# New prices for an offline instruction planner, and other places for the turns of the small expert groups

## The chip, the cores and the metric

The kernel runs on one core of a Trainium2 chip. The metric is the device time of one whole execution in microseconds (us), as the median of the runs. One execution was also taken by the hardware profiler; all rows and windows below are from it. Engines: PE is TensorE, DVE is VectorE, ACT is ScalarE, POOL is GpSimd, SP is SyncE; PEld is TensorE's weight load.

## The reference

The input x has 4 sequences of 1024 steps with 256 channels. Two residual blocks follow each other; LN is a layer norm without weights.

```python
x = x + LN(rec(LN(x)))        # px = h@Ws.T + bs; g = sigmoid(h@Wg.T + bg)
                              # state_t = tanh(px_t + state_{t-1});  out_t = g_t * state_t
x = x + LN(ffn(LN(x)))
# ffn: h = rms(x, n1_w); q, k, v of 16 heads of 16 columns; q, k rms-normed per head
#      x1 = x + causal_attention(q, k, v) @ wo.T      (first 64 columns of the addend are 0)
#      xf = rms(x1, n2_w); softmax gate over 4 experts, the best 2 kept, weights normed to 1
#      e0: gelu(xf@up)@down    e1: (silu(xf@w1) * (xf@w2))@down
#      e2: four layers with gelu    e3: three layers with gelu
#      return x1 + sum of the experts by weight       (first 64 columns of the addend are 0)
```

The recurrence over 1024 time steps is serial: each step adds and takes a tanh of 4 x 256 numbers.

## The kernel before

**Tiling.** Time is cut into 8 chunks of 128 steps (`NI`), each with all 4 sequences, so attention has 32 tiles `(i, b)` of 128 queries. After attention, each token's row goes to DRAM (`row_d`) and its number to the list of one of 6 expert pairs ("kinds", in the `order` 3, 0, 1, 2, 4, 5). Each kind is worked off in groups of 256 tokens, gathered from DRAM by index. What is left of a kind, at most 128 tokens, is its "tail": a small group of its own, run behind all kinds, under a branch on the count. In this run two of the six tails have tokens.

**Order.** Nothing is scheduled by the compiler here. The kernel is written as some twenty generators ("streams"), which yield `Op(engine, cost, prio, reads, slots, banks, lag, ahead)` before they issue an instruction. `Plan.run` keeps one waiting `Op` of each stream and picks the one with the least start time, less its `ahead`, then the least `prio`. It then moves that engine's planned clock:

```python
key = (t - op.ahead, op.prio, n)
...
self.clock[op.eng] = t + op.cost
self.end = t + op.cost + op.lag
```

`end` is when the result counts as ready for readers and for the buffers given back. So `cost` and `lag` (us) settle nothing but the order in which instructions stand on each engine; on the chip each engine runs its list in that order and waits for semaphores. The planner also knows the buffers (`slots`) and the 7 PSUM banks, and places an instruction only where it believes one free. `fill` puts small bf16 matmuls with no use but to keep PE busy (L417) into planned PE gaps of 0.8 us and more, between 60 and 420 us of planned time.

**Streams around the change**, in the order in which a chunk passes through them:
- projections (L534) and gates (L567): products for px and g, transposed input by `transposed` (L463, copies L472).
- `recurrence`: per step a POOL add (L583) into `s` and an ACT tanh (L586), with the best priority, -9.
- `before`: gated state, transposed into `pu` (L623), two layer norms (`moments` L447; rows L643), x1 in one of two `xns` buffers (also called xn), row to DRAM.
- `heads`: q, k product `pqk` (L711), pad copy (L718), squares (L724), norm product (L739), transposes (L798), copies of k (L751) and q (L762). `value_rows` makes v (L778, L787).
- scores: per step of up to 4 blocks of 128 keys, products "s" (queries by keys, for the row maxima) and "sT" (keys by queries, for exp), both L883, with `ahead` 0.3. `look_maxima`: DVE reduces (L968, L975).
- exps (L1024, ACT, up to 512 columns), masks on the diagonal (L1044, POOL), products av with v (L1065).
- `after`, per tile: av copied (avT, L1084), transposed on PE (L1091), divided (L1096, L1098), transposed (L1109), copied (L1114), product with wo (L1120), added into xn, which gives x2 (L1128). An `xns` buffer is given back when all four tiles of its chunk have passed here and `experts_input`.
- `experts_input`: squares (L1142), transposes, gate product, weights and row to DRAM; then the counts of each kind and the lists.
- experts: `fetch` (POOL indirect DMA, L1516), `turn` (DVE scale x, L1531; PE transposes T, L1538; ACT copy, L1544), `group` with products up (L1561) and down (L1581), activations (L1622 to L1638), outputs (DVE, L1649), and `last`: layer norm and add (L1662 to L1678), rows to `out` (POOL indirect DMA, L1681). A group's plan holds its own pieces and a list `then`: the next groups' fetches and turns. Its up products read what its own turn, planned in the group before, made. `turn` uses one PSUM bank for all, and a tail's turn uses the same buffer for x as the turn of a kind's first group. `groups` chooses `then`; further groups of a kind are nested in a branch (L1728), tails in the branches of L1742.

Of the kernel before, what the change touches and what calls it, by code (L numbers as in the profile page):

```python
# [15 lines left out]
PSUM = bass.MemoryType.PSUM  # L16
# [237 lines left out]
def sandwich(  # L254
# [188 lines left out]
    def moments(prio, tiles, tag, reads):  # L443

        mv = stat.tile([P, len(tiles), 2], F32, tag=tag, name=tag)
        for n, t in enumerate(tiles):
            yield Op("DVE", 0.6, prio, reads)  # L447
            st6 = stat.tile([P, 6], F32, tag="st6", name="st6")
            nc.vector.bn_stats(st6, t)
            nc.vector.bn_aggr(mv[:, n, :], st6)  # L450
        return mv

    def transposed(prio, srcs, reads, name, ahead=0.0):


        n = len(srcs)
        big_, *bs = yield Op(
            "PE", 0.25 * n + 0.1, prio, reads, [big], banks=NCC, lag=0.2, ahead=ahead
        )
        to = big.tiles[big_[1]]  # L460
        for cc in range(NCC):
            for b, src in enumerate(srcs):
                nc.tensor.transpose(  # L463
                    banks.tiles[bs[cc]][:, b * P : (b + 1) * P],
                    src[:, cc * P : (cc + 1) * P], ident,
                )
        done(name, "in PSUM")
        for cc, (eng, copy) in enumerate(
            (("ACT", nc.scalar.copy), ("DVE", nc.vector.tensor_copy))
        ):  # L470
            yield Op(eng, 0.65, prio, [ev(name, "in PSUM")])
            copy(to[:, cc, : n * P], banks.tiles[bs[cc]][:, : n * P])  # L472
            give(bs[cc])
            done(name, cc)
        return big_, [ev(name, cc) for cc in range(NCC)]
# [94 lines left out]
    def recurrence():  # L570

        prev = None
        for i in range(NI):
            st, _ = states(i)
            last = ev("st", i)
            for t in range(P):
                if prev is None:
                    yield Op("ACT", 0.21, -9.0, [last])
                    nc.scalar.activation(st[:, :, t], st[:, :, t], AF.Tanh)
                else:  # L580
                    yield Op("POOL", 0.21, -9.0, [last])
                    s = sp.tile([P, NCC * B], F32, tag="s", name="s")
                    nc.gpsimd.tensor_tensor(s, st[:, :, t], prev, ALU.add)  # L583
                    done("s")
                    yield Op("ACT", 0.21, -9.0, [ev("s")])
                    nc.scalar.activation(st[:, :, t], s, AF.Tanh)  # L586
                    if t == 0:
                        done("last read", i - 1)
                done("t")
                last = ev("t")  # L590
                prev = st[:, :, t]
                if t == MOST - 1:
                    done("most", i)
            done("rec", i)
# [5 lines left out]
    def before():  # L600


        for i in range(NI):
# [34 lines left out]
                r = power(z, "r1")  # L638
            done("r1", i)
            for b in range(B):  # L640
                row, = yield Op("DVE", 0.8, prio, [ev("r1", i), ev("x1in", i)], [rows])
                t = rows.tiles[row[1]]
                nc.vector.tensor_scalar(  # L643
                    t, pu[b], mv[:, b, 0:1], r[:, b : b + 1], ALU.subtract, ALU.mult
                )
                nc.vector.tensor_tensor(x1[:, b, :], t, x1[:, b, :], ALU.add)
                give(row)
                if b % 2:
                    give(pu_b[b // 2])
# [44 lines left out]
    def heads(i, bs):  # L694
# [9 lines left out]
        for k, b in enumerate(bs):  # L704
            pad, pb = yield Op(
                "PE", 1.9, prio, [*hT_, ev("once")], [pads], banks=1, lag=0.2
            )
            pad_of[i, b] = pad
            pqk = banks.tiles[pb]
            for cc in range(NCC):  # L710
                nc.tensor.matmul(  # L711
                    pqk, lhsT=hT[:, cc, b * P : (b + 1) * P], rhs=wqk[:, cc, :],
                    start=(cc == 0), stop=(cc == NCC - 1),
                )
            done("pqk", i, b)
            qk = pads.tiles[pad[1]].rearrange("p s h d -> p (s h) d")[:, :, 0:HD]
            yield Op("ACT", 0.69, prio, [ev("pqk", i, b)])
            nc.scalar.activation(  # L718
                qk, pqk.rearrange("p (h d) -> p h d", d=HD), AF.Copy, scale=r3[:, b : b + 1]
            )  # L720
            give(pb)
            sq_, = yield Op("ACT", 0.62, prio, (), [sqs])
            sq = sqs.tiles[sq_[1]]
            nc.scalar.activation(sq, qk, AF.Square)  # L724
            done("sq", i, b)
            if len(bs) > 1:
                yield from value_rows(i, b)
            yield Op("DVE", 0.62, prio, [ev("sq", i, b)])
            nc.vector.tensor_reduce(ss[:, k * 2 * H : (k + 1) * 2 * H], sq, AX.X, ALU.add)
            give(sq_)  # L730
# [2 lines left out]
        rq = newton(ss, f"rq{n}")  # L733
        for k, b in enumerate(bs):
            if len(bs) > 1:
                yield Op("DVE", 0.8, prio + b)
            pad = pads.tiles[pad_of[i, b][1]]
            qk = pad.rearrange("p s h d -> p (s h) d")[:, :, 0:HD]
            nc.vector.tensor_tensor(  # L739
# [5 lines left out]
            pb, = yield from heads_T(prio + b, pad, 1, [ev("pad", i, b)])  # L745
            done("pk", i, b)
            yield Op(
                "ACT", 0.69, prio + b,
                [ev("pk", i, b), *([ev("last read", i)] if i < NI - 1 else [])],
            )  # L750
            nc.scalar.activation(  # L751
                kT[:, b, :, i * P : (i + 1) * P],
# [5 lines left out]
            q, pb = yield from heads_T(prio + b, pad, 0, [ev("pad", i, b)], [qs])  # L758
            give(pad_of[i, b])
            done("pq", i, b)  # L760
            yield Op("ACT", 0.69, prio + b, [ev("pq", i, b)])
            nc.scalar.activation(  # L762
                qs.tiles[q[1]], banks.tiles[pb].rearrange("p (h q) -> p h q", q=P),
                AF.Copy, scale=qn_s,
# [7 lines left out]
    def value_rows(i, b):  # L772
        prio = 4.0 * i - 5.0
        to, hT_, r3 = hT_of[i]
        pb, = yield Op("PE", 1.0, prio, hT_, banks=1, lag=0.2)
        pv = banks.tiles[pb][:, : H * HD]
        for cc in range(NCC):
            nc.tensor.matmul(  # L778
                pv, lhsT=big.tiles[to[1]][:, cc, b * P : (b + 1) * P], rhs=wv[:, cc, :],
                start=(cc == 0), stop=(cc == NCC - 1),  # L780
            )
        done("pv", i, b)
        values_of[i] = values_of.get(i, 0) + 1
        if values_of[i] == B:
            give(to)
        yield Op("DVE", 0.46, prio, [ev("pv", i, b)])
        nc.vector.tensor_scalar(  # L787
            v_all[:, b, i, :, 0:HD], pv.rearrange("p (h d) -> p h d", d=HD),
            r3[:, b : b + 1], None, ALU.mult,
        )  # L790
        give(pb)
        done("v", i, b)
# [153 lines left out]
    def look_maxima():  # L946

        for step in steps:
# [7 lines left out]
            for p in (1, 0):  # L956
                for j in range(2):
                    for m0, m1, h0, h1, half in step.runs:
                        yield Op(
                            "DVE", 0.12 + 1.05e-3 * (m1 - m0) * P, step.at - 1.05,  # L960
                            [ev("s", step.key, p)],
                        )
                        pb = of_step["s", step.key, p][j]
                        if not step.added and step.blocks[m1 - 1][1] == i:
# [47 lines left out]
    def exps():  # L1012
        for step in steps:
            of_step["ex", step.key] = []
            for p in range(2):
                ex = None
                for j in range(2):
                    got = yield Op(
                        "ACT", 0.2 + 0.83e-3 * step.w, step.at, [ev("sT", step.key, p)],
                        [] if ex else [exs],  # L1020
                    )
                    ex = ex or got[0]
                    pb = of_step["sT", step.key, p][j]
# [7 lines left out]
    def masks():  # L1031
        for step in steps:
            for p in range(2):
# [1 line left out]
                    continue  # L1035
                m, _, several = step.diagonal
                for j in range(2) if several > 1 else (slice(0, 2),):
                    yield Op("POOL", 0.72 if several > 2 else 0.42, step.at, [ev("e", step.key, p)])
                    e = exs.tiles[of_step["ex", step.key][p][1]][:, j, : step.w]
                    if several > 1:  # L1040
                        d, pattern = on_diagonal(e, step), [[0, several], [1, P]]
# [35 lines left out]
    def after(ns):  # L1077

        for n in ns:
            i, b = tiles[n]  # L1080
            prio = n + 1.5
            ahead = GATES_FIRST if n == NT - 1 else 0.0
            yield Op("DVE", 0.69, n - 0.5, [ev("av", n)])
            nc.vector.tensor_copy(avT, av)  # L1084
            done("av free", n)
            row, pb = yield Op(
# [3 lines left out]
            for hc in range(NHC):  # L1090
                nc.tensor.transpose(pa[:, hc * P : (hc + 1) * P], avT[:, hc, :], ident)  # L1091
            done("pa", n)
            yield Op("DVE", 0.7, prio, [ev("pa", n)])
            pa = pa.rearrange("p (h d) -> p h d", d=32)
            rs = stat.tile([P, H, 1], F32, tag="rs", name="rs")
            nc.vector.reciprocal(rs, pa[:, :, HD : HD + 1])  # L1096
# [12 lines left out]
                nc.tensor.transpose(pt[:, cc, :], ao[:, cc * P : (cc + 1) * P], ident)  # L1109
            give(row)  # L1110
            done("aoT0", n)
            yield Op("ACT", 0.39, prio, [ev("aoT0", n)])
            aoT = tees.tiles[to[1]]
            nc.scalar.copy(aoT, pt)  # L1114
            give(pb)
# [7 lines left out]
                )  # L1123
            give(to)
            done("po", n)
            yield Op("DVE", 0.36, prio, [ev("po", n)])
            xn = xns.tiles[xn_of[i][1]]
            nc.vector.tensor_tensor(xn[:, b, M:], po, xn[:, b, M:], ALU.add)  # L1128
            give(pb)
# [2 lines left out]
    def experts_input(chunks):  # L1132

        for i in chunks:
# [2 lines left out]
            xn = None  # L1137
            ss = stat.tile([P, B], F32, tag="ss2", name="ss2")
            for b in range(B):
                row, = yield Op("ACT", 0.6, prio, [ev("x2", i, b)], [rows])  # L1140
                xn = xns.tiles[xn_of[i][1]]
                nc.scalar.activation(  # L1142
                    rows.tiles[row[1]], xn[:, b, :], AF.Square, accum_out=ss[:, b : b + 1]
# [256 lines left out]
def experts(  # L1400
# [294 lines left out]
    def groups(c, g):  # L1695
# [6 lines left out]
        then = [fetch(c, g + 2)]  # L1702
        if g == 0:
            then += [fetch(kind(n + 2), 0), fetch(kind(n + 2), 1)]
            for before in [order[n - 1]] if n else []:
                then.append(fetch(before, TAIL, 1.0))
            if n + 1 == KINDS:
                then.append(fetch(c, TAIL, 1.0))
            else:
                then.append(turn(kind(n + 1), 0))  # L1710
        if more:
            then.append(turn(c, g + 1))
# [27 lines left out]
    for n, c in enumerate(order):  # L1740
        hint(f"tail{n}", KINDS + c, 0)
        with tc.If(n_of[KINDS + c] > 0, preferred_fallthrough_block=True, label=f"tail{n}"):  # L1742
            group(c, TAIL, [turn(c, TAIL)])


# [57 lines left out]
```

## Time and profile before

| what | value |
|---|---|
| median of 3 runs | 1471.9 us (1470.63 to 1476.9) |
| profiled execution | 1470.96 us |
| its span, first to last instruction | 1469.2 us |
| mean granted TensorE clock | 0.947 |
| PE busy | 1311.5 us, 89% |
| DVE, ACT, POOL busy | 896.5, 705.7, 465.5 us |
| fillers (L417) on PE | 38.6 us |
| recurrence, first to last tanh | 17.6 to 741.0 us |
| first exp to last exp | 147.7 to 1028.3 us |
| first tail's x to the end | 1426.94 us to 1469.2 us |

Some 1.8 us of the execution lie around the span. In a row of a profile, the source line and engine come first, then output and inputs by their names in the program, shapes, the count, busy time, the mean of one in ns, and the idle time of the engine before these instructions with what ended most of it. In a timeline the start and the duration come first. In windows the stretch, its length, and for each engine its busy time with the count, then the granted TensorE clock as a share of full speed. Matmuls may be merged into one line where they follow each other.

### The profile page before, as it was taken

Reading aid. Unit: us, or ns where it says so; the run is one execution under the profiler, and the core shown is the slowest. Engines: PE = TensorE matmul, PEld = TensorE weight load, DVE = VectorE, ACT = ScalarE, POOL = GpSimd, SP = SyncE. Lnnn points to the kernel's source line nnn. Section 1 sums busy time; section 2 is a strip of 40 time slices with the busy share of each in tenths; the row PEclk is TensorE's granted clock in tenths of the full one; section 3 lists DMA queues with packets and bytes.
Section 4 is the critical chain, followed back from the end, with each engine's and each line's share of the span. In section 5 each row is a group of like instructions: output and inputs, shape, how many; then the busy total and the mean of one; then the engine's idle time right before and its main releaser. Section 6 shows DMA issues by size and latency. Waiting matters only on the chain. (4 is left out here: it accounts for less than half of the span.)

```text
span 1469.2 us, 43267 instructions
## 1 busy us (share of the span) xinstructions
PE 1311.5 (89%) x17455; PEld 1020.3 (69%) x17470; DVE 896.5 (61%) x2738; ACT 705.7 (48%) x2144; POOL 465.5 (32%) x1466
## 2 busy tenths in 40 slices
PE   4578797988999998999999999999899999999964
PEld 2235455666676676687677677878688889888764
DVE  5567568599688778778877987784614312113311
ACT  2345545655765765776665455657222222223211
POOL 2433534535444444334311101101233321214321
PEclk8799989999998989998999999999999999999987
DMA  3010010001010000001000100131122120103210
GB/s 128 23 50 2 4 42 17 16 3 46 3 31 17 3 22 28 3 3 46 3 4 5 45 3 4 38 105 62 55 84 64 54 66 26 40 23 83 55 43 5
DMA packets 35917, 49.57 MB, mean 34 GB/s; under 512 B 7638, under 2 KB 27862, under 8 KB 35670
## 3 DMA queue, kind: packets, MB, share of 16 engines
q1 hardware_dynamic: 28774, 25.20, 5.6%
q0 software_dynamic: 6624, 20.62, 5.0%
q8 instruction: 147, 2.41, 0.7%
q14 instruction: 100, 0.82, 0.2%
q10 hardware_dynamic: 272, 0.52, 0.1%
HBM read 32.87 MB, written 13.46 MB: 32 GB/s over the span
## 5 line engine op out<-in xcount | busy, mean ns | idle before, releaser
L1024 ACT ACTIVATE ex<-bank 128x512 f32<-128x512 f32 (+1 forms) x592 | 325.9, 582 | 153.4 <-PE bank L883 87.5
L883 PE MATMUL bank<-keys,q 32*128 32x128 f32 x4608 | 351.9, 293 | 17.4 <-ACT q L762 4.1
L583 POOL TENSOR_TENSOR s<-keys 128x8 f32<-128x8 f32 x1023 | 223.4, 218 | 384.8 <-ACT keys L586 374.1
L883 PE MATMUL bank<-q,keys 32*128 32x128 f32 x4608 | 333.9, 292 | 5.4 <-ACT ex L1024 2.8
L883 PEld LDWEIGHTS bank<-q,keys 32*128 32x128 f32 x4608 | 272.6, 191 | 75.7 <-issue 41.9
L586 ACT ACTIVATE keys<-s 128x8 f32<-128x8 f32 x1023 | 218.5, 214 | 212.1 <-POOL s L583 209.5
L883 PEld LDWEIGHTS bank<-keys,q 32*128 32x128 f32 x4608 | 292.2, 193 | 37.0 <-DVE nm L975 6.3
L975 DVE TENSOR_REDUCE nm<-bank 128x1 f32<-128x512 f32 (+4 forms) x336 | 203.0, 639 | 53.7 <-PE bank L883 44.5
L968 DVE CUSTOM_DVE_ANT_0 bank<-bank,late 128x512 f32<-128x512 f32 (+2 forms) x320 | 188.3, 622 | 48.7 <-PE bank L883 47.4
L1044 POOL TENSOR_SCALAR_AFFINE_SELECT ex<-ex 128x256 f32<-128x256 f32 (+1 forms) x240 | 102.7, 429 | 262.4 <-ACT ex L1024 261.4
L1065 PE MATMUL av<-ex,values 128*17 128x128 f32 x4608 | 175.0, 282 | 3.1 <-issue 1.2
L1561 PE MATMUL bank<-values,keys 128*128 128x256 f32 x568 | 133.5, 381 | 5.9 <-PEq L1728 3.0
L1065 PEld LDWEIGHTS av<-ex,values 128*17 128x17 f32 x4608 | 110.0, 99 | 40.3 <-issue 16.4
L1622 ACT ACTIVATE keys<-bank 128x256 f32<-128x256 f32 (+1 forms) x136 | 50.4, 371 | 149.8 <-PE bank L1561 149.7
L1561 PEld LDWEIGHTS bank<-values,keys 128*128 128x128 f32 x568 | 105.8, 190 | 21.7 <-issue 3.5
L1561 PE MATMUL bank<-keys 128*128 128x256 f32 x384 | 84.8, 379 | 0.0
L1561 PEld LDWEIGHTS bank<-keys 128*128 128x128 f32 x384 | 73.0, 190 | 9.9
L534 PE MATMUL bank<-big,wsg 128*128 128x512 f32 x128 | 64.0, 646 | 5.9 <-ACT big L472 5.9
L711 PE MATMUL bank<-wqk,big 128*128 128x512 f32 x128 | 65.7, 642 | 3.2 <-ACT big L472 3.2
L1649 DVE SCALAR_TENSOR_TENSOR rwnext<-av,rwnext 128x192 f32<-128x192 f32 x24 | 8.9, 414 | 93.4 <-PE av L1581 93.4
L1622 ACT ACTIVATE hid<-bank 128x256 f32<-128x256 f32 x66 | 25.3, 383 | 84.5 <-PE bank L1561 84.5
L1669 POOL TENSOR_SCALAR z<-mv 128x2 f32<-128x2 f32 (+1 forms) x18 | 4.1, 227 | 187.7 <-DVE mv L1663 178.4
(265 smaller groups left out, 1788.2 us busy)
## 6 DMA issues: line engine op xcount, KB each, us to landing
row_d<-xn SPq DMA_DIRECT2D x16, 512.0 KB
xn<-in_x SPq DMA_DIRECT2D x8, 512.0 KB
xc<-in_x SPq DMA_DIRECT2D x7, 512.0 KB
keys<-in_e_l SPq DMA_DIRECT2D x2, 1024.0 KB
keys<-in_e_w SPq DMA_DIRECT2D x2, 512.0 KB
keys<-in_e_down SPq DMA_DIRECT2D x2, 384.0 KB
wsg<-in_w_sg ACTq DMA_DIRECT2D x1, 512.0 KB
xc<-in_x SPq DMA_DIRECT2D x4, 128.0 KB
```

The source lines that it names most:

```text
L534: nc.tensor.matmul(pb, lhsT=wsg[:, cc, half * C + dc * P : half * C + (dc + 1) * P], rhs=lnT[:, cc, :], start=(cc == 0), stop=(cc == NCC - 1),
L583: nc.gpsimd.tensor_tensor(s, st[:, :, t], prev, ALU.add)
L586: nc.scalar.activation(st[:, :, t], s, AF.Tanh)
L711: nc.tensor.matmul(pqk, lhsT=hT[:, cc, b * P : (b + 1) * P], rhs=wqk[:, cc, :], start=(cc == 0), stop=(cc == NCC - 1),)
L883: nc.tensor.matmul(banks.tiles[pbs[j]][:, m * P : (m + 1) * P], lhsT=k if kind == "sT" else q, rhs=q if kind == "sT" else k, start=(m == 0 ...
L968: nc.vector.tensor_tensor_reduce(out=s_, in0=s_, in1=late[:, 4 * P - w :], scale=-1.0, scalar=FMAX, op0=ALU.add, op1=ALU.min, accum_out=by ...
L975: nc.vector.tensor_reduce(by_slot[:, half, h0:h1, 2 * p + j], banks.tiles[pb][:, m0 * P : m1 * P].rearrange("p (h w) -> p h w", h=h1 - h0) ...
L1024: nc.scalar.activation(exs.tiles[ex[1]][:, j, : step.w], banks.tiles[pb][:, : step.w], AF.Exp)
L1044: nc.gpsimd.affine_select(out=d, in_=d, pattern=pattern, compare_op=ALU.is_ge, fill=0.0, base=0, channel_multiplier=-1,)
L1065: nc.tensor.matmul(av[32 * j : 32 * j + HD + 1, hc, :], lhsT=v_all[:, b, kb, 4 * hc + j, :], rhs=exs.tiles[ex[j // 2][1]][:, j % 2, m * P ...
L1561: nc.tensor.matmul(hb[0].tiles[hb[1]][:, :w_], lhsT=w[:, j, m * P : (m + 1) * P], rhs=src[:, j, :w_], start=(j == 0), stop=(j == nk - 1),)
L1622: nc.scalar.activation(to, src, AF.Gelu)
```

## The change

**Prices.** The costs of the ACT, DVE and POOL pieces of the first part of the kernel (up to the experts' lists) are lowered, a few raised, and a `lag` is added to most, so that what an instruction occupies its engine and what passes until its result can be read count apart. PE's prices, the priorities and the dependencies stay. The expert groups' own prices stay too.

**Turns of the tails.** Before, the first group of each kind but the first fetched the rows of the tail of the kind before (the last kind also its own), and each tail's own group began with its turn. After, in the first group of the kind at place n of the order: n = 1 fetches the tails of the places 0, 1 and 2; n from 2 on that of place n + 1. Their turns are planned there as well: n = 2 turns tails 0 and 1, n = 3 tail 2, n = 4 tail 3, n = 5 tails 4 and 5. All six are turned, whether the tail has tokens or not, and a tail's group holds no turn.

The diff, with the places between left out:

```diff
-            yield Op("DVE", 0.6, prio, reads)
+            yield Op("DVE", 0.53, prio, reads, lag=0.08)
...
-            yield Op(eng, 0.65, prio, [ev(name, "in PSUM")])
+            yield Op(eng, 0.5, prio, [ev(name, "in PSUM")], lag=0.1)
...
-                    yield Op("POOL", 0.21, -9.0, [last])
+                    yield Op("POOL", 0.16, -9.0, [last], lag=0.07)
-                    yield Op("ACT", 0.21, -9.0, [ev("s")])
+                    yield Op("ACT", 0.11, -9.0, [ev("s")], lag=0.11)
...
-                row, = yield Op("DVE", 0.8, prio, [ev("r1", i), ev("x1in", i)], [rows])
+                row, = yield Op("DVE", 0.92, prio, [ev("r1", i), ev("x1in", i)], [rows], lag=0.08)
...
-            yield Op("ACT", 0.69, prio, [ev("pqk", i, b)])
+            yield Op("ACT", 0.58, prio, [ev("pqk", i, b)], lag=0.1)
-            sq_, = yield Op("ACT", 0.62, prio, (), [sqs])
+            sq_, = yield Op("ACT", 0.55, prio, (), [sqs], lag=0.1)
...
-                yield Op("DVE", 0.8, prio + b)
+                yield Op("DVE", 0.61, prio + b, lag=0.08)
...
-                "ACT", 0.69, prio + b,
-                [ev("pk", i, b), *([ev("last read", i)] if i < NI - 1 else [])],
+                "ACT", 0.58, prio + b,
+                [ev("pk", i, b), *([ev("last read", i)] if i < NI - 1 else [])], lag=0.1,
...
-            yield Op("ACT", 0.69, prio + b, [ev("pq", i, b)])
+            yield Op("ACT", 0.58, prio + b, [ev("pq", i, b)], lag=0.1)
...
-        yield Op("DVE", 0.46, prio, [ev("pv", i, b)])
+        yield Op("DVE", 0.39, prio, [ev("pv", i, b)], lag=0.07)
...
-                            "DVE", 0.12 + 1.05e-3 * (m1 - m0) * P, step.at - 1.05,
-                            [ev("s", step.key, p)],
+                            "DVE", 0.1 + 1.0e-3 * (m1 - m0) * P, step.at - 1.05,
+                            [ev("s", step.key, p)], lag=0.08,
...
-                        "ACT", 0.2 + 0.83e-3 * step.w, step.at, [ev("sT", step.key, p)],
-                        [] if ex else [exs],
+                        "ACT", 0.05 + 0.84e-3 * step.w, step.at, [ev("sT", step.key, p)],
+                        [] if ex else [exs], lag=0.12,
...
-                    yield Op("POOL", 0.72 if several > 2 else 0.42, step.at, [ev("e", step.key, p)])
+                    yield Op("POOL", 0.6 if several > 2 else 0.37, step.at, [ev("e", step.key, p)], lag=0.1)
...
-            yield Op("DVE", 0.69, n - 0.5, [ev("av", n)])
+            yield Op("DVE", 0.6, n - 0.5, [ev("av", n)], lag=0.08)
...
-            yield Op("DVE", 0.7, prio, [ev("pa", n)])
+            yield Op("DVE", 0.62, prio, [ev("pa", n)], lag=0.08)
...
-            yield Op("ACT", 0.39, prio, [ev("aoT0", n)])
+            yield Op("ACT", 0.27, prio, [ev("aoT0", n)], lag=0.12)
...
-            yield Op("DVE", 0.36, prio, [ev("po", n)])
+            yield Op("DVE", 0.27, prio, [ev("po", n)], lag=0.08)
...
-                row, = yield Op("ACT", 0.6, prio, [ev("x2", i, b)], [rows])
+                row, = yield Op("ACT", 0.4, prio, [ev("x2", i, b)], [rows], lag=0.1)
...
         then = [fetch(c, g + 2)]
         if g == 0:
             then += [fetch(kind(n + 2), 0), fetch(kind(n + 2), 1)]
-            for before in [order[n - 1]] if n else []:
-                then.append(fetch(before, TAIL, 1.0))
-            if n + 1 == KINDS:
-                then.append(fetch(c, TAIL, 1.0))
-            else:
+
+            if n:
+                got = range(3) if n == 1 else (n + 1,)
+                turned = {2: (0, 1), KINDS - 1: (KINDS - 2, KINDS - 1)}.get(n, (n - 1,) if n > 1 else ())
+                then += [fetch(kind(k), TAIL, 1.0) for k in got]
+                then += [turn(kind(k), TAIL) for k in turned]
+            if n + 1 < KINDS:
         if more:
...
         with tc.If(n_of[KINDS + c] > 0, preferred_fallthrough_block=True, label=f"tail{n}"):
-            group(c, TAIL, [turn(c, TAIL)])
+            group(c, TAIL, [])
```

## The prediction, made before the changed kernel ran

> **What bounds the kernel now.** I read the page's busy times and costliest groups first, then stretches of the span, then the recurrence's line alone in the same stretches, then the timeline at the group boundaries that the second part of the change touches.
>
> ```profile
> PE 1311.5 (89%) x17455; PEld 1020.3 (69%) x17470; DVE 896.5 (61%) x2738; ACT 705.7 (48%) x2144; POOL 465.5 (32%) x1466
> L1024 ACT ACTIVATE ex<-bank 128x512 f32<-128x512 f32 (+1 forms) x592 | 325.9, 582 | 153.4 <-PE bank L883 87.5
> L583 POOL TENSOR_TENSOR s<-keys 128x8 f32<-128x8 f32 x1023 | 223.4, 218 | 384.8 <-ACT keys L586 374.1
> L586 ACT ACTIVATE keys<-s 128x8 f32<-128x8 f32 x1023 | 218.5, 214 | 212.1 <-POOL s L583 209.5
> ```
>
> PE is busy 89%, an average over stages that differ. The 1023 steps of the recurrence alternate between POOL (L583) and ACT (L586): each waits for the other. With nothing else on ACT in between, one step takes 0.522 us in the trace. The stretches below are cut at exps (L1024): first exp of a time chunk to its last ("chunk"), and last exp to the next chunk's first ("gap").
>
> ```profile
> core 0: us, PE busy (x) PEld busy (x) DVE busy (x) ACT busy (x) POOL busy (x), PEclk, DMA share, GB/s
> 159.30:245.60 86.30, 67.79 (x477) 43.52 (x479) 62.70 (x216) 42.88 (x177) 33.98 (x147) 0.90 0.09 26
> 292.80:323.60 30.80, 27.13 (x346) 18.78 (x346) 28.50 (x89) 16.33 (x68) 12.55 (x54) 1.00 0.01 2
> 424.10:521.20 97.10, 90.39 (x1603) 68.48 (x1605) 76.83 (x244) 64.50 (x216) 43.34 (x157) 0.93 0.07 19
> 531.80:645.00 113.20, 106.82 (x2016) 81.24 (x2016) 89.34 (x267) 75.40 (x248) 45.16 (x172) 0.93 0.06 17
> 645.00:647.00 2.00, 1.56 (x36) 1.26 (x32) 1.81 (x4) 1.44 (x6) 0.98 (x4) 1.00 0.03 8
> ```
>
> In a chunk PE is 93 to 94% busy. In the gap 159.3 to 245.6 it is idle for 18.5 us, filler matmuls included. The gap at 645 hardly exists. The recurrence alone in the gaps (first number behind the window is its length, then ACT busy with its count):
>
> ```profile
> 159.30:245.60 86.30, 30.54 (x143) 0.90 0.09 26
> 292.80:323.60 30.80, 11.15 (x53) 1.00 0.01 2
> 645.00:647.00 2.00, 0.47 (x3) 1.00 0.03 8
> ```
>
> So a gap is as long as the steps ordered into it: 143 steps x 0.522 plus what other ACT operations add makes 85.2 (measured 86.3); 53 make 31.8 (30.8). Gaps of few steps are those in which attention of the next chunk was ready.
>
> **Part A, the prices.** Durations do not change, nor any instruction's count (fillers aside): only the order. The new prices are near what the trace shows start to start (an exp of 512 columns 476 ns, now 0.48 for 0.625; the pad copy 570 to 585, now 0.58). PE's prices, among them 1.9 for L711's product, stay. So the question is what order results, and I take it from the instruction lists of both kernels. Recurrence steps between the last exp of a chunk and the first of the next, chunk 0 first: before 143, 53, 40, 20, 3, 0, 0; after 166, 41, 113, 2, 93, 0, 0. Exps ahead of the last step: 298 before, 240 after, of 592. The reason is in the order too: with cheap exps and reduces, scores (which have 0.3 us of "ahead") are always ready first, and PE work between the last av product of a tile and its avT transposes grows from 3.5 to 12 us in the median. So x2 is done later, xn's two slots come free later, and the next chunks' heads come late: the first L718 of chunk 3 is at step 585 where it was at 548, of chunk 5 at 919 for 820. In those gaps PE has only heads, projections and leftovers.
>
> Price of the gaps after: steps x 0.522 plus the trace's mean surplus for each ACT operation between steps (L718 0.91, L724 0.15, L751 0.35, L762 0.37, L1142 0.29, L472 0.31, L1114 0.33, L567 0.2, L1191 0.15). Gap 0: 86.7 + 11.9 for 33 operations = 99. Gap 1: 25 by steps, 32.5 us of PE work, so 33. Gap 2: 59.0 + 11.5 for 30 operations = 70. Gap 3: 1. Gap 4: 48.5 + 8.8 for 23 = 57. The last two 2.5 and 1. Sum 264, measured before 154: +110. Without any surplus the gaps after sum to 232: +78.
>
> Price of the chunks: PE work (each matmul at its busy time in the trace, 894 us in all, the same in both) moves from chunks to gaps. In the eight chunks it was 6.7, 41.9, 65.8, 88.7, 104.4, 121.9, 142.5, 114.8 (686.7; they took 726.4, so 39.7 us are stalls); it becomes 6.7, 33.0, 50.3, 78.7, 80.4, 107.8, 147.8, 109.5. At each chunk's own ratio these take 11, 37, 59.4, 86.2, 87.1, 112.3, 146, 106.8 = 645.8: -80.6. So gaps and chunks net +29, or -3 at the bare pace.
>
> Covers: PE work between first score product and sT grows from 9.4 to 14.9 us in the median, and cases with under 1.5 us between an exp and its av fall from 8 to 5. With fewer steps in the chunks this can take some of the 39.7 us of stalls; the ratio has already taken 8, and I give another 12 (rather under a third), with 0 and 25 as bounds. Against it, the cover between the gate's product and the counts falls from 26.4 to 1.9 us, and that chain takes 5.8 us in the trace (1043.78 to 1049.60): +4. Part A: 29 - 12 + 4 = +21. The fillers go from 154 to 159; 37 now stand together behind chunk 0's first transposes, 10.3 us at the 0.28 us that one keeps PE busy (38.6 us / 139 records), in a wait of 14.7 us for the row norms (90.8 to 105.5): nothing, unless that wait shrank by 4.
>
> The row 159.3 to 245.6, a gap with idle PE, has the clock 0.90; the packed one at 292.8 has 1.00. [...]
>
> **Part B, the turns.** Read at kind 2's first group, and at the two tails that run:
>
> ```profile
> 1187.27 0.60 PE L1538 MATMUL bank<-ident,values 128*128 128x128 f32 x4
> 1187.47 0.74 DVE L1649 SCALAR_TENSOR_TENSOR rwfirst<-bank,rwfirst 128x192 f32<-128x192 f32 x2 [2.64 <-PE bank L1581]
> 1187.91 0.58 ACT L1544 COPY values<-bank 128x512 f32<-128x512 f32 x1 [2.45 <-PE bank L1538]
> 1188.55 1.13 PE L1561 MATMUL bank<-values,keys 128*128 128x256 f32 x4 [0.67 <-ACT values L1544]
> 1426.94 0.35 DVE L1531 TENSOR_SCALAR values<-rwtail 128x256 f32<-128x256 f32 x1 [5.63 <-DVEq L1742]
> 1427.44 0.66 PE L1538 MATMUL bank<-ident,values 128*128 128x128 f32 x2 [10.95 <-DVE values L1531]
> 1428.13 0.37 ACT L1544 COPY xtail<-bank 128x256 f32<-128x256 f32 x1 [13.77 <-PE bank L1538]
> 1442.21 0.66 PE L1538 MATMUL bank<-ident,values 128*128 128x128 f32 x2 [3.65 <-DVE values L1531]
> ```
>
> Turns share one bank and, in part, one buffer, and the next kind's own turn already stands last in the group. Kind 2's last down product ends at 1187.27, and the next product starts 1.28 later. After, the order at this end is on PE T2, down, T2, T4, T4, on DVE x, outputs, x2, moments, x2 (T2, T4: transposes of one or two tiles). So behind the last down come outputs 0.74, moments 0.53, x 0.61, T4 0.60, copy 0.59, then x, T4 and copy again (1.80): with hops about 5.35, +4.1. Kind 3: T2, down, T4, T4 for T4, down, T4: 3.3 for 1.33, +2.0. Kind 4 +0.25, the last kind +0.6. Sum +6.95. Three row fetches more than one needs in kind 1 (9 for 7, 1.27 us of POOL each) delay rows by 2.5 us that have 6 in hand: nothing.
>
> Gains: at the first tail PE has walked the untaken branches by 1425.03, and DVE, ACT and PE then need x, T and copy until 1428.56. Without them a product can start at 1425.7: -2.85. At the second, PE is done with the first tail at 1438.57, but DVE's x waits behind that tail's closing chain until 1441.71, and the first product starts at 1443.33: -4.76. Together -7.6. Part B: -0.7, between -6 (turns hidden) and +2.
>
> **Sum.** The profiled execution took 1470.96, 0.9 below the median 1471.9. 1470.96 + 21 - 0.7 = 1491.
>
> **Rivals.** 0.5%, 7.4 us, is about what a measurement of this kernel can tell from no change.
> (1) Forecast: starved gaps lengthen the attention by more than the chunks return. Surplus full or half, stalls 0 to 25 off: 1482 to 1504. 0.62.
> (2) Faster: the surplus of ACT operations is mostly waiting on PE (L718 waits for L711) or contention that thinner stretches lack, so gaps run bare (-3), and the chunks lose a third or more of their 40 us of stalls (-12 to -20), the tails give their -1 to -6: 1450 to 1462. It decides if the gaps' steps come under 0.54 us. For it: the smallest surplus of an exp is 0.05, its mean 0.26. 0.13.
> (3) No net change, gaps bare and nothing more, or a cancelling of both: 1466 to 1479. 0.12.
> (4) Worse: the sum of the chunks is too kind, because their PE stalls do not shrink with their work (+8 on the ratio), and idle gaps cost clock (0.90 instead of 1.00 on 90 us of PE work in gaps 2 and 4: +9): 1505 to 1512. 0.13.
> The range 1464 to 1508 leaves out most of (2) and half of (4). Likeliest case alone: 1482 to 1504.
>
> **What would show it.** Right: some 113 tanh steps and 70 us between the exps of chunks 2 and 3, 93 steps and 57 us between 4 and 5, PE idle there for 15 to 25 us each; chunk 5's first exp near 690 (was 647), though the recurrence ends near 690 (was 741); attention's last exp near 1050 (was 1028); kind 2's first group 4 us longer; first tail product 2.9 and second 4.8 us sooner than the kinds' end would give. Wrong: gap steps at 0.53 us, or chunks 4 to 6 shorter than 87, 112 and 146 us.

## The result, and the profile after

| | median us | ratio to the kernel before, 95% interval |
|---|---|---|
| before | 1471.27 (4 runs) | |
| after | 1496.34 (4 runs) | 1.0163 [1.0141, 1.0185] |

The change costs 25 us. The profiled execution of after took 1495.79 us with a span of 1494.0 (before 1469.2), PE is busy 1335.6 us of it, again 89%, and the mean clock is 0.939 (0.947). The 24.7 us between the spans divide at the last exp: 17.5 ahead of it (1045.9 us, before 1028.3), 7.2 behind.

The stretches of after, cut at the exps as in the prediction (columns as there): the gaps behind chunks 0, 2 and 4, and between the last two, chunk 3.

```profile
core 0: us, PE busy (x) PEld busy (x) DVE busy (x) ACT busy (x) POOL busy (x), PEclk, DMA share, GB/s
157.70:253.90 96.20, 78.28 (x552) 49.34 (x552) 71.86 (x236) 48.68 (x204) 40.56 (x172) 0.93 0.08 23
377.20:448.20 71.00, 55.81 (x495) 39.43 (x487) 55.05 (x190) 36.63 (x148) 30.94 (x120) 0.86 0.09 24
448.20:528.70 80.50, 79.03 (x1596) 60.64 (x1600) 62.78 (x177) 58.84 (x203) 36.80 (x147) 0.96 0.01 3
618.30:678.80 60.50, 50.23 (x493) 38.05 (x491) 49.85 (x140) 29.25 (x121) 26.54 (x100) 0.77 0.09 28
```

The gap behind chunk 2 was 22.7 us and is 71.0; that behind chunk 4 was 2.0 and is 60.5. PE is idle for 15.2 and 10.3 us of them (the first numbers, less PE's busy time). Chunk 3 with the gap ahead of it paid is 98% busy. The recurrence alone (window, ACT busy with its count, clock) has 113 and 93 steps in these gaps:

```profile
377.20:448.20 71.00, 23.91 (x113) 0.86 0.09 24
618.30:678.80 60.50, 19.71 (x93) 0.77 0.09 28
```

Why the next chunk wasn't ready is seen in SP's queue: the row of chunk k - 2 goes out with x2 (L1149), and only when its transposes have read it can the load of chunk k (L607) take the same xn buffer. First the kernel before, for chunks 3 and 5, then after (start, duration of the issue):

```profile
332.39 0.36 SPq L1149 DMA_DIRECT2D row_d<-xn  x1
336.89 0.38 SPq L607 DMA_DIRECT2D xn<-in_x  x1
...
544.60 0.43 SPq L1149 DMA_DIRECT2D row_d<-xn  x1
548.92 0.38 SPq L607 DMA_DIRECT2D xn<-in_x  x1
```

```profile
341.16 0.36 SPq L1149 DMA_DIRECT2D row_d<-xn  x1
354.78 0.38 SPq L607 DMA_DIRECT2D xn<-in_x  x1
...
563.32 0.37 SPq L1149 DMA_DIRECT2D row_d<-xn  x1
580.83 0.53 SPq L1006 DMA_DIRECT2D q<-top  x1
581.47 0.52 SPq L607 DMA_DIRECT2D xn<-in_x  x1
```

Chunk 3's load comes 17.9 us later, chunk 5's 32.6. Of the latter 18.7 are a later x2, and 13.8 the longer way from the row to the load (18.2 us for 4.3): the transposes of x2 stand late in PE's list too (L463, at 579.8 us; before at 547.3). SP's own list adds little: q<-top (L1006), which stands ahead of the load, is issued at 580.83, just as the transposes end. All exps of chunk 4 are through at 618.3, but chunk 5's first product L711 needs x1, and its first pad copy (L718) is at 609.0 (before 578.1).

Behind the last exp, the end of kind 2's first group (timeline: start, duration; in brackets the engine's idle time and what ended it):

```profile
1208.76 0.38 PE L1538 MATMUL bank<-ident,values 128*128 128x128 f32 x2
1209.18 0.37 ACT L1544 COPY xtail<-bank 128x256 f32<-128x256 f32 x1 [2.41 <-PE bank L1538]
1210.24 0.61 DVE L1531 TENSOR_SCALAR values<-rwfirst 128x256 f32<-128x256 f32 x2
1210.74 0.72 PE L1538 MATMUL bank<-ident,values 128*128 128x128 f32 x4 [1.60 <-DVE values L1531]
1212.14 1.08 PE L1538 MATMUL bank<-ident,values 128*128 128x128 f32 x4 [0.68 <-ACT values L1544]
1213.90 1.65 PE L1561 MATMUL bank<-values,keys 128*128 128x256 f32 x3 [0.68 <-ACT values L1544]
```

The chain is the one foretold: the transposes right behind the last down product start at 1208.76, and the next product starts 5.1 us later (before 1.28). What follows was not foretold; the windows of the same place, clock third from the right:

```profile
1206.00:1210.00 4.00, 3.14 (x21) 2.88 (x19) 1.39 (x4) 1.02 (x3) 0.00 (x0) 1.00 0.00 0
1210.00:1214.00 4.00, 1.90 (x9) 1.24 (x9) 2.94 (x11) 1.17 (x2) 1.14 (x3) 0.78 0.00 0
1214.00:1218.00 4.00, 4.00 (x10) 3.19 (x11) 1.10 (x3) 0.67 (x2) 1.76 (x2) 0.50 0.09 33
1218.00:1222.00 4.00, 4.00 (x18) 3.46 (x17) 0.00 (x0) 1.25 (x4) 2.22 (x3) 0.87 0.43 120
```

PE is full from 1213.90 on, but the clock is halved (0.50): 10 matmuls of L1561 in 4 us, where the same line has 20 from 1222.00 to 1226.00, at a clock of 1.00. Cut more finely, the granted clock is 1.00 up to 1212.2, 0.50 from 1212.3 to 1219.0, in the middle of the chain and behind it, and 1.00 again from 1219.1 on. Before, the clock is 1.00 from 1180 to 1204 us, around the same end.

A last place, in kind 1's first group, where three tails are fetched:

```profile
1153.51 0.95 POOL L1516 DMA_INDIRECT rwtail<-row_d,tails  x1 [0.30 <-issue]
...
1155.57 0.41 DVE L1675 TENSOR_SCALAR rwfirst<-rwfirst,mv,r 128x256 f32<-128x256 f32 x1 [6.68 <-POOL r L1670]
...
1157.41 0.41 DVE L1632 SCALAR_TENSOR_TENSOR tnext<-tnext,bank 128x256 f32<-128x256 f32 x1
...
1157.87 4.97 PE L1561 MATMUL bank<-values,keys 128*128 128x256 f32 x20 [2.27 <-DVE tnext L1632]
```

POOL issues the last fetch, then makes r of the layer norm; DVE waits 6.68 us for r with the norm and x, and the piece that takes the tanh of the *next* products (L1632) stands behind them in DVE's list. PE waits 2.27 us for that.

### The profile page after: what moved, and what is told of

It is laid out like the page before. It is cut to its first block, busy times and chain, and to the rows that moved or that the text cites. A ratio compares the mean times of both kernels' runs of the same rounds, so it can differ in the third digit from the quotient of the medians.

```text
span 1494.0 us, 43375 instructions
## 1 busy us (share of the span) xinstructions
PE 1335.6 (89%) x17483; PEld 1039.6 (70%) x17483; DVE 900.7 (60%) x2742; ACT 709.1 (47%) x2148; POOL 468.5 (31%) x1466
## 5 line engine op out<-in xcount | busy, mean ns | idle before, releaser
L1024 ACT ACTIVATE ex<-bank 128x512 f32<-128x512 f32 (+1 forms) x592 | 320.3, 582 | 140.2 <-PE bank L883 71.3
L883 PE MATMUL bank<-q,keys 32*128 32x128 f32 x4608 | 320.0, 290 | 7.8 <-ACT ex L1024 5.2
L883 PEld LDWEIGHTS bank<-q,keys 32*128 32x128 f32 x4608 | 261.7, 189 | 74.5 <-issue 40.8
L975 DVE TENSOR_REDUCE nm<-bank 128x1 f32<-128x512 f32 (+4 forms) x336 | 202.8, 639 | 52.2 <-PE bank L883 42.3
L1561 PE MATMUL bank<-values,keys 128*128 128x256 f32 x568 | 139.6, 394 | 6.7 <-PEq L1730 2.9
L1561 PEld LDWEIGHTS bank<-values,keys 128*128 128x128 f32 x568 | 109.8, 197 | 24.8 <-issue 3.4
L1561 PE MATMUL bank<-keys 128*128 128x256 f32 x384 | 84.8, 379 | 0.0
L1561 PEld LDWEIGHTS bank<-keys 128*128 128x128 f32 x384 | 73.0, 190 | 9.9
L711 PE MATMUL bank<-wqk,big 128*128 128x512 f32 x128 | 66.3, 643 | 2.9 <-ACT big L472 2.3
```

The lines of the kernel that those rows point to most:

```text
L711: nc.tensor.matmul(pqk, lhsT=hT[:, cc, b * P : (b + 1) * P], rhs=wqk[:, cc, :], start=(cc == 0), stop=(cc == NCC - 1),)
L883: nc.tensor.matmul(banks.tiles[pbs[j]][:, m * P : (m + 1) * P], lhsT=k if kind == "sT" else q, rhs=q if kind == "sT" else k, start=(m == 0 ...
L975: nc.vector.tensor_reduce(by_slot[:, half, h0:h1, 2 * p + j], banks.tiles[pb][:, m0 * P : m1 * P].rearrange("p (h w) -> p h w", h=h1 - h0) ...
L1024: nc.scalar.activation(exs.tiles[ex[1]][:, j, : step.w], banks.tiles[pb][:, : step.w], AF.Exp)
L1561: nc.tensor.matmul(hb[0].tiles[hb[1]][:, :w_], lhsT=w[:, j, m * P : (m + 1) * P], rhs=src[:, j, :w_], start=(j == 0), stop=(j == nk - 1),)
```

## The experiments

Each ratio is taken against runs of the kernel before on the same chip in the same session. It took 1473 to 1485 us in those sessions, so medians are not compared between them; times expected below count from the 1471 us of the result and are read by the ratio.

**The two parts apart.** One kernel has the new prices with the old choice of tails, the other the old prices with the new choice:

```diff
 # the prices alone: the lines of groups() and of the tails' branch as before
-            group(c, TAIL, [])
+            group(c, TAIL, [turn(c, TAIL)])
 # the turns alone: every Op(...) price as before
-                yield Op("ACT", 0.11, -9.0, [ev("s")], lag=0.11)
+                yield Op("ACT", 0.21, -9.0, [ev("s")])
...
```

> The new prices with the tails as before. Theory G (starved gaps): the order of the attention is that of the changed kernel, with 166, 41, 113, 2 and 93 recurrence steps between the exps of successive chunks, so the last exp comes 17 to 18 us later than before, near 1046 us, and the expert stage is as before: about 1489 us. Rival T (the tails' turns and what they do to the clock make most of the loss): under 1480 us.

> The old prices with the tails turned inside later kinds' groups. The attention's order is that of before, so the last exp stays near 1028 us. Theory G with what the changed kernel's trace shows of the expert stage (2.9 us at kind 1 behind three fetches, about 6 at kind 2, 1.9 at kind 3, 1 to 2 at kind 4 from a lower clock, 1.8 and 5.6 back at the two tails): 1474 to 1479 us. My prediction's sum for this part, -0.7, would give 1471. Rival T: over 1482 us.

Measured: the prices alone 1.0127 [1.0103, 1.0152], with 113 and 93 steps in gaps of 72.5 and 61.2 us and the last exp at 1047.8 us. The turns alone 1.0035 [1.0019, 1.0051], last exp at 1027.9. Together 1.0162, the changed kernel 1.0163: the parts add, and three quarters are the prices'.

**Is it the gaps?** Two ways of removing them that keep (nearly) all new prices:

```diff
 # prices, after() ahead (all prices new)
-            ahead = GATES_FIRST if n == NT - 1 else 0.0
+            ahead = GATES_FIRST if n == NT - 1 else 0.3
 # prices, old steps (the recurrence's two prices old)
-                    yield Op("POOL", 0.16, -9.0, [last], lag=0.07)
-                    yield Op("ACT", 0.11, -9.0, [ev("s")], lag=0.11)
+                    yield Op("POOL", 0.21, -9.0, [last])
+                    yield Op("ACT", 0.21, -9.0, [ev("s")])
```

> All new prices, tails as before, and the PE pieces of the stream behind attention (avT, aoT and wo products of each tile) get the same 0.3 us of ahead as the scores. In the instruction lists the steps between the chunks' exps become 159, 51, 32, 27 and 6, so none of the two big gaps is left, though each price is new. Theory G: 1466 to 1476 us, near before. Rival P (the new prices cost through shorter covers everywhere, not through the gaps): 1483 us or more, as with the prices alone.

> All new prices but the two of the recurrence's steps (0.21 for the POOL add and for the tanh, no lag), tails as before. The instruction lists then have 139, 58, 40, 2 and 6 steps between the chunks' exps. Theory G: no starved gap, 1463 to 1475 us. Rival P: 1483 us or more. If the recurrence's own prices alone made the loss, this would be at or under 1471 too; the run before this one tells that apart, since it keeps them.

Measured: 1.0019 [1.0005, 1.0033] and 0.9983 [0.9962, 1.0005]. Both take away nearly all of the 1.27%. The first ended its exps even at 1023.5, 4.9 us ahead of before, and gave that back at once (its time is 1.0019), since the gate of chunk 6 now stood behind the last av products with nothing beside it:

```profile
1030.43 0.62 PE L1214 MATMUL bank<-kind,earlier 128*128 128x24 f32 x2 [4.50 <-DVE kind L1201]
...
1034.98 3.33 PE L1258 MATMUL bank<-row,tee 128*128 128x192 f32 x8 [3.50 <-DVE row L1248]
```

So I gave, besides, the experts' input the 1.0 of ahead that only its last chunk had:

```diff
-            ahead = GATES_FIRST if i == NI - 1 else 0.0
+            ahead = GATES_FIRST if i == NI - 1 else 1.0
```

> All new prices, tails as before, the stream behind attention 0.3 ahead and the experts' input 1.0 ahead for all chunks (before for the last only). Steps between the chunks' exps 162, 54, 36, 6, 6. The gate's product of chunk 6 no longer stands at the end of attention, where the run with 0.3 ahead alone lost 4.5 + 3.5 us of idle PE. Theory G: the last exp at or before 1028 us and those 8 us gone: -4 to -10 us against before. Rival P: no gain, equal to the run with 0.3 ahead alone (+3).

Measured 0.9998 [0.9977, 1.002]: the two idle pieces are gone, but no time is gained on before; rival P, not theory G, had that. The last exp is at 1037.2, with gate and rows ahead of it, the first kind's transposes follow at once (1038.3; before 1041.0), and PE then waits 8.44 us in that group, in a place where it had not waited in the traces of before and after, and 4.4 to 7.1 us in all other experiments but one. What part of the 8.44 is this kernel's is not shown.

**Is it the xn buffer?** A third xn buffer needs room, so a buffer of exps and one of a tanh were taken away, with two and with three xn buffers:

```diff
-    xns = slots(2, [P, B, C], "xn")
+    xns = slots(3, [P, B, C], "xn")        # not in the control
-    exs = slots(6, [P, 2, 4 * P], "ex", ip)
+    exs = slots(5, [P, 2, 4 * P], "ex", ip)
-    ts = {w: slots(2, [P, N], "t" + w) for w in both}
+    ts = {w: slots(1 if w == "first" else 2, [P, N], "t" + w) for w in both}
```

> All new prices, tails as before, three xn buffers for two; to make room one buffer less for exps (five for six) and one less for the silu pair's tanh of the first groups. Nothing is given priority. In the instruction lists the steps between the chunks' exps become 150, 43, 27, 6, 2: both starved gaps go. Theory X (late x2 holds an xn buffer, so the next chunks' heads wait): near before, within 0.5%. Rival P (prices cost through covers, or fewer exp buffers cost): 0.8% slower or more.

> The control to the run before: the same new prices and the same two buffers less, but two xn buffers as ever. Steps between the chunks' exps 150, 40, 63, 2, 134: one gap of some 63 x 0.64 = 40 us and one of 134 x 0.66 = 88 us. Theory X: 1.0 to 1.6% slower than before. Rival P: equal to the run before.

Measured: three buffers 0.9847 [0.982, 0.9874], two 1.0094 [1.0063, 1.0125]. One buffer more is worth 2.4% under the new prices, and the kernel with it beats the kernel before too, where I had expected it within 0.5% of it: 1461.8 us beside 1485.1 on that chip. Its loads no longer wait for the row that goes out:

```profile
285.94 0.43 SPq L607 DMA_DIRECT2D xn<-in_x  x1
341.84 0.43 SPq L1149 DMA_DIRECT2D row_d<-xn  x1
```

and its gaps behind chunks 2 and 4 are 13.8 and 0.8 us, packed:

```profile
401.40:415.20 13.80, 12.98 (x218) 9.73 (x214) 13.73 (x45) 5.90 (x30) 5.79 (x28) 1.00 0.01 3
640.10:640.90 0.80, 0.80 (x23) 0.68 (x17) 0.71 (x2) 0.22 (x3) 0.57 (x2) 1.00 0.03 10
```

The control has them at 41.2 and 85.4, PE busy 86 and 73%:

```profile
385.90:427.10 41.20, 35.45 (x407) 28.33 (x397) 31.55 (x94) 21.36 (x87) 17.11 (x67) 0.80 0.09 27
596.90:682.30 85.40, 62.08 (x521) 45.60 (x520) 68.80 (x232) 42.14 (x170) 36.67 (x144) 0.76 0.10 26
```

Over all seven gaps, three buffers have 134.4 us, before 154.1, the chunks 726.0 and 726.4: the last exp comes at 1008.3, 20 us sooner, and all of it is gaps. Is that the buffer or the prices? The same three lines in the kernel before:

> The kernel before (old prices, tails as before) with the same three changes of buffers as the run of three xn buffers: xn three for two, exps five for six, one tanh buffer less. Steps between the chunks' exps 143, 48, 41, 27, 3 (before: 143, 53, 40, 20, 3), so by theory X nothing waits for an xn buffer under the old prices: within 0.5% of before, and the 1.5% that new prices with three buffers gained come from the prices, once the buffer is there. Rival Y (the third buffer is the gain, whatever the prices): 1.0% faster or more.

Measured 1.0 [0.9985, 1.0014]. The buffer alone (with the two that make room for it) is worth nothing, the prices alone cost 1.3%, and the two together gain 1.5%.

**The turns.** Their cost in the changed kernel sits at the ends of groups, so, with all prices old, I gave PE's transposes of a tail a better priority, then also spread the fetches as before:

```diff
-        yield Op("PE", 0.6, 5.0, [ev("xs", c, g, t) for t in range(nt)], lag=0.2)
+        yield Op("PE", 0.6, soon, [ev("xs", c, g, t) for t in range(nt)], lag=0.2)
...
-                then += [turn(kind(k), TAIL) for k in turned]
+                then += [turn(kind(k), TAIL, 0.5) for k in turned]
 # spread: one fetch and one turn for a kind, two for the last
-                got = range(3) if n == 1 else (n + 1,)
+                then.append(fetch(order[n - 1], TAIL, 1.0))
...
```

> The old prices, the tails' rows fetched and turned in the same groups as in the changed kernel, but PE's transposes of a tail get priority 0.5 for 5.0. In the instruction lists they then stand amid a group's products, and the group ends in T4, down, T4 as before the change. Theory E (the turns cost because they stand at the end of a group, where nothing is left for PE, and the idle time there halves PE's clock for a few us): kind 2's and kind 3's 8 us go, the 2.9 at kind 1 behind three fetches stay, the tails give 7.4 back: 0.1 to 0.4% faster than before (-2 to -6 us). Rival F (the fetches, or six turns done for two tails that need them, are the cost): at or above the time of before, as with the turns alone (+5).

> As the run before, and the tails' fetches as before the change, one for a kind and two for the last; the turns one for a kind, two for the last, the last tail's in its own group. Theory: the 2.9 us of PE behind DVE at kind 1 go as well: 2 to 3 us under the run before, -4 to -8 us against before. If the three fetches cost nothing, as my prediction had it, the two runs are equal.

Measured 1.0021 [0.9994, 1.0047] and 0.9992 [0.9969, 1.0015]; neither came out faster than before, and the first is where rival F had it. The stretches between transposes say where the gain went. From those ahead of kind 2's first group to those of its second: before 55.0, turns alone 61.1, early 56.5, early and spread 56.3. In kind 1's first group: 19.9, 24.0, 24.8 and 20.5, so spreading the fetches takes 4.3 us off there: the three fetches do cost, in that place. But around kind 3's first group it is 30.9, 32.7, 33.4 and 33.1, and the last kind's went from 26.6 to 28.2 and 28.0. Kind 3 in the run with early turns:

```profile
1342.84 2.75 PE L1561 MATMUL bank<-hid,values 128*128 128x256 f32 x12
1347.20 0.44 PE L1538 MATMUL bank<-ident,values 128*128 128x128 f32 x2 [1.61 <-DVE values L1531]
```

```profile
1343.78 0.43 DVE L1678 TENSOR_TENSOR rwnext<-rwnext 128x256 f32<-128x256 f32 x1
1346.79 0.35 DVE L1531 TENSOR_SCALAR values<-rwtail 128x256 f32<-128x256 f32 x1 [2.59 <-issue]
```

The transposes now stand early in the group, and so does their wait: DVE comes to the tail's x only when it has closed the group before (1344.2) and entered this one (2.59 us in which the profile names nothing that it waits for). Theory E was right about kind 2, where 4.6 of the 6.2 us are gone, and wrong as a recipe: at kind 3, too early is as bad as last.

**The clock.** Four fillers ahead of the transposes that wait for x at kind 2's end, in the kernel with the turns alone:

```diff
+    FILL_AT, FILL_N = {0: (3,)}, 4
...
+        if turn_of[c] in FILL_AT.get(g, ()):
+            yield Op("PE", 0.0, 5.0, [ev("xs", c, g, t) for t in range(nt)])
+            for _ in range(FILL_N):
+                nc.tensor.matmul(
+                    tb[0].tiles[tb[1]].rearrange("p k n -> p (k n)"), lhsT=route["ident_h"],
+                    rhs=route["late"], start=True, stop=True,
+                )
         yield Op("PE", 0.6, 5.0, [ev("xs", c, g, t) for t in range(nt)], lag=0.2)
```

> The turns alone (old prices) with 4 small bf16 matmuls in PE's list at the end of kind 2's first group, ahead of the transposes that wait for x there; nothing else moves. In the changed kernel this place had 2.96 us of idle PE in pieces and a granted clock of 0.78, 0.50 and 0.87 in the 12 us behind it; the time from the first tail transposes there to those of the next group was 33.9 us (27.7 before). Theory C (the idle pieces drop the clock): the clock stays at 1.00 and the stretch falls to 31 to 32.5 us, fillers and all. Rival: the stretch stays at 33.9 or grows by the fillers' 0.9 us.

Measured, in the one execution of this kernel: 31.0 us for 33.9 (1200.20 to 1231.17), with the chain of x, transposes and copies still there, and the clock at 1.00 from 1196 to 1216 us:

```profile
1204.00:1208.00 4.00, 2.56 (x12) 1.31 (x12) 2.95 (x11) 1.17 (x2) 1.10 (x2) 1.00 0.00 0
1208.00:1212.00 4.00, 4.00 (x20) 3.51 (x20) 1.38 (x4) 1.54 (x4) 1.51 (x2) 1.00 0.09 33
```

So of the 6.2 us that kind 2's end costs in these traces, 2.9 are the clock and 3.3 the chain.

But the half clock in kind 4's first group is not shown to be the order's doing. PE has the same products there before and after, and the same waits among them (0.62, 0.53 and 1.83 us); here the products behind the last of these waits, before and then after:

```profile
1373.65 1.99 PE L1561 MATMUL bank<-hid,values 128*128 128x256 f32 x8 [1.83 <-DVE tfirst L1632]
```

```profile
1403.30 3.68 PE L1561 MATMUL bank<-hid,values 128*128 128x256 f32 x8 [1.83 <-DVE tfirst L1632]
```

These eight products take 1.99 us at a clock of 1.00, or 3.68 at 0.54. The kernel with the prices alone, whose groups are those of before, has 3.64 in its trace, and the one with the turns and the four fillers at kind 2 has 1.99. So in these four traces the 1.7 us come once with the turns and once without them, and are not shown to be the turns'.

**All together**, the changed kernel with both aheads and early, spread turns:

> The changed kernel with the two aheads and the early, spread turns, all of the above together. If the parts add: the sum of the two runs before this one, -8 to -18 us against before.

Measured 0.9973 [0.9951, 0.9996]: 4 us under before, half of the least that I hoped for, since neither part brought its gain (0.9998 and 0.9992 alone). The third buffer does more with three lines.

## Why the prediction was right, point by point

The forecast of 1491 us was for starved gaps that lengthen attention by more than the chunks return. That is what came, through the gaps and not beside them: the two experiments that remove the gaps and keep the prices (all of them, or all but the steps') remove the loss, and so does a third xn buffer.

- **Gaps.** +110 predicted (264), +103.2 measured (257.3). One by one: 99, 33, 70, 1, 57, 2.5, 1 predicted; 96.2, 25.6, 71.0, 0.8, 60.5, 2.2, 1.0 measured. Steps times 0.522 plus the mean surplus of each ACT operation was a good price, and the idea that gaps run bare (rivals 2 and 3) fell: 0.634 and 0.657 us from tanh to tanh in the two big ones. The gap behind chunk 1 came out at the 25 of its steps and not at the 33 of PE's work; PE is busy for 24.8 of its 25.6 us, so which of the two bound it is not shown, but the 32.5 us of work were counted too high. In the gap behind chunk 4 PE is idle for 10.3 us, under the 15 to 25 foretold, and chunk 5 starts at 678.8, not near 690.
- **Chunks.** -92.6 predicted with the 12 us for better covers, -84.3 measured (642.1). The fixed ratio alone gave -80.6. That leaves 4 for the covers, but no run shows them apart, and one by one the chunks lie up to 10 us off the ratio: 45.5 for 37 (chunk 1), 52.2 for 59.4, 80.5 for 86.2, 88.8 for 87.1, 102.3 for 112.3, 151.4 for 146. Chunk 5, under its 112, is one of the signs of being wrong that the prediction had named. That the sum fits better than its terms is luck.
- **First exp and gate.** The first exp came 1.2 us sooner, not in the sum. The gate's chain was priced at +4 and cost 0.2 in the changed kernel; in the kernel with after() ahead PE is idle for 8.0 us of it.
- Gaps, chunks and start make 17.7 us, my own sum 17 without the gate. The gaps were 7 us too large and the chunks' gain 8; that they cancel is luck as well.
- **Turns.** -0.7 predicted, 7.2 measured behind the last exp, and this is the part that I had wrong, sign included. Kind 2's end: 4.1 predicted, 6.2 measured; the chain alone is 3.3, the rest is half clock. I had weighed the clock for the gaps only, where it does fall (0.86 and 0.77) but PE still has 15.2 and 10.3 us of waiting left; at kind 2's end, with PE full behind the chain, it cost 2.9 us. Kind 1's three fetches: "nothing" predicted, 2.9 measured; I had looked at the slack of x and not at DVE's tanh piece queued behind the norm that POOL delays. Kind 3's end 1.8 (2.0 predicted). Kind 4's group 1.7 (0.25 predicted), all of it the half clock (3.68 us for 1.99 in eight products) that is not shown to be the turns'. The first kind's group 1.1, the last kind 0.8 with its way to the tails. The tails: -1.8 for -2.85, and -5.6 for -4.76 (-4.8 of it up to the second tail's first product).

A sum of 20 for 24.8 us is thus a good price of attention, helped by terms that cancel, and an 8 us miss at the turns. 1496 lies in the likeliest case's 1482 to 1504, so the mechanism was right and the breadth given to the surplus and the stalls covered the turns.

## What to carry to other kernels

Prices of an offline planner settle only an order; true prices can give a worse one when some other limit (here two xn buffers) had been kept harmless by the false ones. Read from the order what each stage will have to do beside a serial chain, and price the stretch by the chain's steps; then ask which buffer made the next stage late, because freeing that one may turn the loss into the gain. A piece moved into a full engine's list cost time here both last in it (6.2 us at kind 2's end) and ahead of what feeds it (33.4 us for 30.9 around kind 3's first group), and in POOL's queue the fetches delayed what stood behind them (DVE waits 6.68 us for r where it waited 2.46 before; 2.9 us in kind 1's first group): look at both ends of the place, and at every queue that the piece is put into.

## What the runs showed of the hardware

At kind 2's end PE is idle for 1.60 and 0.68 us within 3.0 us (after); at 1212.2 the clock falls from 1.00 to 0.50 and stays so until 1219.0, though PE has work all along from 1213.90 on. In the run with the four fillers at that place (0.46, 0.68 and 0.68 us idle) it stays at 1.00. In kind 4's group the clock halves behind a stretch that is as busy (after):

```profile
1208.80:1212.20 3.40, 1.12 (x8) 0.62 (x7) 2.81 (x10) 0.96 (x2) 0.54 (x2) 1.00 0.00 0
1212.30:1219.00 6.70, 6.02 (x16) 4.64 (x16) 2.26 (x6) 1.36 (x3) 2.95 (x4) 0.50 0.08 30
1399.95:1403.30 3.35, 1.13 (x5) 0.68 (x5) 0.67 (x3) 0.71 (x2) 1.02 (x2) 1.00 0.12 42
1403.40:1406.70 3.30, 3.30 (x8) 2.65 (x9) 0.11 (x1) 0.38 (x1) 0.63 (x1) 0.50 0.13 45
```

Before, the same stretch of kind 4 did not halve it:

```profile
1370.30:1373.65 3.35, 1.13 (x4) 0.68 (x5) 0.67 (x3) 0.71 (x2) 0.99 (x2) 1.00 0.13 44
1373.75:1377.05 3.30, 3.30 (x17) 2.97 (x18) 0.80 (x3) 0.77 (x2) 0.67 (x1) 1.00 0.13 45
```

So with PE busy for 1.1 us of some 3.4 the clock fell to 0.50 behind two of these three stretches and stayed at 1.00 behind the third; what decides it is not shown by these runs. At kind 2's end PE was never idle for longer than 1.60 us at a time, so a list of PE's gaps over that length doesn't find this place, and the granted clock in short windows does.

Until the clock was back at 1.00, PE was busy without a pause for 5.1 us at kind 2's end (1213.90 to 1219.0) and for some 3.4 at kind 4 (1403.30 to 1406.7).

In the sessions in which the kernel before took 1483 to 1485 us, every trace has a wait of PE of 4.4 to 8.4 us in the first kind's group, ahead of L1561 and mostly put down to "issue"; in the two sessions with 1471 and 1473 us no trace has it, the second of them on a chip that had shown it before. The profile names no cause, and no run here was made for it.
